# A graph layer on one core: the first messages ahead of a later pair's sum, and a read-back that ends twelve steps beyond the last chunk

## The chip, the core and the metric

The kernel runs on one core of a Trainium2 chip. The metric is the device time of one execution in microseconds (us). A change of less than 0.2% (about 8.5 us here) is taken as no change.

The core has five engines that each work through a queue of their own in order: TensorE (PE, with its weight loads shown as PEld), VectorE (DVE), ScalarE (ACT), GpSimd (POOL) and SyncE (SP, which here issues most DMAs). They wait for each other through semaphores.

## The reference

The layer takes 12,500 nodes of 128 features and 412,500 edges, sorted by `dst`. The part that matters:

```python
h = jnp.maximum(_layernorm(x, axis=-1), 0.0)
h = h @ W_in2f
Wij = ssp(f_ij @ W_f1 + b_f1) @ W_f2 + b_f2      # ssp(z) = softplus(z) - log 2
Wij = Wij * rcut_ij[:, None]
x_ij = h[idx_j] * Wij                            # idx_j = dst: sorted
agg = segment_sum(x_ij, idx_i, 12500)            # idx_i = src: in no order
out = ssp(agg @ W_o1 + b_o1) @ W_o2 + b_o2
return x + out
```

Every edge makes one message of 128 numbers, and the messages are summed by `src`, which comes in no order.

## The kernel before

**Chunks and steps.** The edges are cut into 806 chunks of 512. One step of the main loop (`step(k, units)`) finishes chunk k and starts work on later ones. It writes the order of every engine's queue by hand. Of one chunk's work, the parts that this text needs:

- `hidden` (L653, L656, L657): for a pair of chunks, PE makes z = f·W_f1, and ACT takes |z| and its exponential. There is one PSUM buffer for z. `hidden_log` (L662) is ACT's logarithm, and `hidden_end` (L668) is DVE's sum that ends the softplus of the pair; it is the "pair's sum" of the title, and it frees z for the next pair.
- `blocks`, `rank`, `rank_end` (L673, L692, L697, L717 to L721): a running count on PE, from which DVE works out the row ("slot") of a table that each message goes to. PE's L725 and L692 follow DVE's L697 of the chunk before.
- `window` (L744), `pick` (L772), `picked` (L780): DVE marks, PE gathers and ACT scales the node rows, which gives `hg`.
- `bias` (L757) and `value` (L764): the filter values `v`. ACT's L757 for a later chunk waits for the message that frees its buffer.
- `message` (L789, L791, L795): DVE multiplies v and hg into `o`, and POOL sends it to the table with four indirect DMAs of 128 rows. There are four `o` buffers, of two chunks each; L789 opens one, and waits until the DMAs that last read it are done.

**Segments and read-back.** The chunks are cut into seven segments (352, 160, 120, 56, 56, 32 and 30 chunks), each with a table of its own in HBM. When a segment's last chunk is 9 steps past, a `Collect` reads its table back in units: `load` (L833, an SP DMA), `compare` (L844, DVE), `add` (L857, PE, one unit later) and, after every four blocks of 128 nodes, `keep` (L880, DVE), which adds PE's sum to `agg`. There is one PSUM buffer for that sum. A unit is 3 to 6 tiles of 128 slots.

**When the units run.** Ahead of the loop a plan spreads the units of the first six segments evenly over the steps, with a common end:

```python
at = [seg.c1 + 9 for seg in segs[:-1]]
end = NCH + 6
```

Each segment gets a rate in tiles a step, so that its units fill the steps from its start to the end (or to the next start, where the rate is higher). The loop runs until the last unit's step, beyond chunk 805 if need be. In such steps there is no message, only read-back. After the loop the last segment, whose table is complete only when POOL is done, is read back, and each group of four blocks goes through `finish` (L410 to L434), which makes the output.

**The order within a step** before the change: `rows`, loads, `blocks`, **`end`** (L668), **`window`** (L744), **`message`**, `keep`, `value`, `pick`, `bias`, `picked`, `compare`, `rank`, `hidden`, `log`, `add`, `rank_end`. L668 comes in every second step.

Of the kernel before, what the change touches and what calls it, by code (L numbers as in the profile page):

```python
# [36 lines left out]
def ceil_div(a, b):  # L37
    return -(-a // b)
# [3 lines left out]
def gnn_kernel(  # L42
# [36 lines left out]
    NCH = ceil_div(n_edges, CH)  # L79
# [438 lines left out]
    with tc.tile_pool(name="edge", bufs=2) as edge, tc.tile_pool(  # L518
# [367 lines left out]
        LG, LW, LR, LZ = 12, 6, 6, 4  # L886

        def of(k):
            return groups[k // NCHUNK], k % NCHUNK
# [6 lines left out]
        made = {}  # L896

        def part(name, upto, make):

            for j in range(made.get(name, -1) + 1, min(upto, NCH - 1) + 1):  # L900
                make(*of(j))
                made[name] = j

        def pairs(make):
            return lambda g, c: None if c % 2 else make(g, c)
# [22 lines left out]
        def group(j):  # L928
            if j not in groups and j < NG:
                groups[j] = Group(j)  # L930

        def ranks(j):

            if 0 <= j < NCH:
                g, c = of(j)
                g.rank(c)
                yield
                g.rank_end(c)

        def step(k, units=()):  # L940

            def has(j):
                return 0 <= j < NCH

            group((k + LG) // NCHUNK)
            part("rows", min(k + LW, 2 * k + 3, NEXT if k < NEXT - 3 else NCH), rows)
            for c, u in units:
                c.load(u + AHEAD)  # L950

            part("blocks", min(k + LR + 1, 2 * k + 1), blocks)
            part("end", min(k + LZ - 2, made.get("log", -1)), pairs(hidden_end))
            part("window", k + 2 if k > 0 else k + 1, window)
            if has(k):
                g, c = of(k)
                g.message(c, vs.pop(k), hgs.pop(k))
            for c in owed:
                c.keep()
            owed.clear()  # L960
            if has(k + 1):
                g, c = of(k + 1)
                vs[k + 1] = g.value(c, bs.pop(k + 1))
                ps = psum.tile([P, QT, P], F32, name="picked", tag="v", bufs=3)
                g.pick(c, ats.pop(k + 1), ps)
            if has(k + 2):

                bs[k + 2] = of(k + 2)[0].bias(of(k + 2)[1])
            if has(k + 1):
                hgs[k + 1] = g.picked(c, ps)  # L970
            for c, u in units:
                c.compare(u)
            upto = max(made["rank"], min(k + LR, 2 * k + 1))
            ready = [ranks(j) for j in range(made["rank"] + 1, upto + 1)]
            made["rank"] = upto
            for r in ready[:1]:
                next(r, None)
            part("hidden", k + LZ, pairs(hidden))
            part("log", k + LZ - 1, pairs(hidden_log))
            for c, u in units:  # L980
                if summed:
                    summed[0].add(summed[1])
                summed[:] = c, u
            for r in ready:
                for _ in r:
                    pass
# [18 lines left out]

        at = [seg.c1 + 9 for seg in segs[:-1]]
        work = [sum(seg.tiles(b) for b in range(NBLK)) for seg in segs[:-1]]
        end = NCH + 6
        rate = {}
        while len(rate) < len(at):  # L1010
            n = len(at) - len(rate)
# [3 lines left out]
            end = at[j]  # L1015
# [9 lines left out]
        i, k = 0, todo[0][0]  # L1025
# [43 lines left out]
        with tc.manual_schedule():  # L1069
# [27 lines left out]
            for k in range(-1, max(NCH, max(units) + 1)):  # L1097
                for seg, d in zeros.get(k, ()):
                    seg.clears.append(nc.sync.dma_start(*d).ins.name)
                now = units.get(k, ())  # L1100
                for c, u in now:
                    if u == 0:
                        for i in range(AHEAD):
                            c.load(i)
                step(k, now)

                for m in h:
                    next(m, None)
                if k > NEXT - 3:
                    next(aside, None)  # L1110
# [101 lines left out]
```

## Time and profile before

| | |
|---|---|
| median of 9 runs | 4232.86 us (4226.41 to 4244.69) |
| the profiled execution | 4232.43 us, of which span 4230.6 us |
| busy: PE, DVE, ACT, POOL | 3388.0, 3376.9, 2682.3, 3100.6 us |
| POOL's 3224 indirect DMAs | 961 ns each |
| granted TensorE clock | 0.82 of full in the mean |

The page of the profile gives the busy time of each engine, the costliest groups of instructions (line, engine, operation, what is written from what, how often, busy time, mean of one, and the idle time before them with what ended it), and the chain that ended last. The timeline has one row for an instruction or a run of equal ones: start and length in us, engine and line, and in brackets the idle time ahead of it and what ended that. A row may stand for several instructions (x2). An instruction's printed length is longer than the space that it takes in a queue: VectorE's 0.68 us rows stand 0.60 us apart.

### The profile page before, as it was taken

Reading aid. Unit: us, or ns where it says so; the run is one execution under the profiler, and the core shown is the slowest. Engines: PE = TensorE matmul, PEld = TensorE weight load, DVE = VectorE, ACT = ScalarE, POOL = GpSimd, SP = SyncE. Lnnn points to the kernel's source line nnn. Section 1 sums busy time; section 2 is a strip of 40 time slices with the busy share of each in tenths; the row PEclk is TensorE's granted clock in tenths of the full one; section 3 lists DMA queues with packets and bytes.
Section 4 is the critical chain, followed back from the end, with each engine's and each line's share of the span. In section 5 each row is a group of like instructions: output and inputs, shape, how many; then the busy total and the mean of one; then the engine's idle time right before and its main releaser. Section 6 shows DMA issues by size and latency. Waiting matters only on the chain. (4 is left out here: it accounts for less than half of the span.)

```text
span 4230.6 us, 71871 instructions
## 1 busy us (share of the span) xinstructions
PE 3388.0 (80%) x21576; PEld 2598.7 (61%) x21576; DVE 3376.9 (80%) x6726; ACT 2682.3 (63%) x5490; POOL 3100.6 (73%) x3244
## 2 busy tenths in 40 slices
PE   6777776767787767778888888888888888888878
PEld 4444454444454445467777777777776777767777
DVE  7877766776666666678888888888988998999988
ACT  6676666666666666666666666665666666666635
POOL 5777777777777777777777777777777777777760
PEclk8677666676656665589999999999999999999999
DMA  6656556555444454467787777887778778877667
GB/s 175 202 180 198 176 168 183 156 153 162 130 118 127 121 165 124 112 182 218 235 268 206 219 212 210 254 241 212 213 231 246 231 203 261 240 198 217 191 188 232
DMA packets 515581, 820.80 MB, mean 194 GB/s; under 512 B 177074, under 2 KB 312870, under 8 KB 515186
## 3 DMA queue, kind: packets, MB, share of 16 engines
q1 hardware_dynamic: 411586, 602.85, 50.5%
q0 software_dynamic: 103168, 213.15, 15.3%
q8 instruction: 176, 2.88, 0.3%
q14 instruction: 219, 1.79, 0.1%
q10 hardware_dynamic: 432, 0.13, 0.0%
HBM read 419.09 MB, written 396.64 MB: 193 GB/s over the span
## 5 line engine op out<-in xcount | busy, mean ns | idle before, releaser
L795 POOL DMA_INDIRECT slots<-o,slot x3224 | 3097.4, 961 | 1011.3 <-issue 793.4
L764 PE MATMUL v<-wf,r 128*128 128x128 f32 x6448 | 1138.2, 333 | 336.3 <-ACT v L757 335.1
L764 PEld LDWEIGHTS v<-wf,r 128*128 128x128 f32 x6448 | 1009.4, 238 | 639.4 <-ACT v L757 632.2
L757 ACT ACTIVATE v<-bf 128x512 f32<-128x512 f32 x804 | 478.4, 595 | 1381.0 <-DVE o L791 1378.5
L857 PEld LDWEIGHTS acc<-to,m 128*128 128x128 f32 x8132 | 1050.1, 207 | 344.0 <-DVE agg L880 140.3
L857 PE MATMUL acc<-to,m 128*128 128x128 f32 x8132 | 1125.4, 296 | 115.8 <-DVE agg L880 76.9
L780 ACT ACTIVATE hg<-picked,rcut 128x128 f32<-128x128 f32 x3224 | 908.1, 363 | 59.0 <-PE picked L772 56.4
L653 PE MATMUL z<-f,wf 20*128 20x512 f32 x1612 | 551.8, 760 | 342.2 <-DVE r L668 315.3
L668 DVE SCALAR_TENSOR_TENSOR r<-z,nbf,a 128x1024 f32<-128x1024 f32 x403 | 516.5, 1282 | 314.3 <-ACT a L662 313.0
L844 DVE TENSOR_TENSOR to<-count_ps,m 128x512 f32<-128x512 f32 (+3 forms) x824 | 640.5, 803 | 54.3 <-DMA m<-slots 36.0
L697 DVE TENSOR_REDUCE top<-free 128x4 f32<-128x392 f32 x806 | 447.7, 555 | 203.3 <-PE free L692 201.8
L791 DVE TENSOR_TENSOR o<-v,hg 128x512 f32<-128x512 f32 x806 | 548.3, 680 | 22.8 <-ACT hg L780 21.7
L744 DVE TENSOR_TENSOR at<-count_ps,rel 96x512 bf16<-96x512 f32 x806 | 544.8, 676 | 0.0
L653 PEld LDWEIGHTS z<-f,wf 20*128 20x128 f32 x1612 | 150.0, 214 | 526.2 <-issue 259.7
L662 ACT ACTIVATE a<-a,half 128x1024 f32<-128x1024 f32 x403 | 467.8, 1161 | 0.0
L656 ACT ACTIVATE a<-z,bf 128x1024 f32<-128x1024 f32 x403 | 455.6, 1130 | 5.4 <-PE z L653 5.4
L673 DVE TENSOR_TENSOR inb<-count_ps,blk 128x392 f16<-128x392 f32 x806 | 444.8, 552 | 0.0
L657 ACT ACTIVATE a<-a 128x1024 f32<-128x1024 f32 x403 | 425.9, 1057 | 12.8
L772 PE MATMUL picked<-near,at 96*128 96x128 bf16 x3224 | 377.9, 250 | 4.0 <-DVE at L744 3.9
L725 PE MATMUL free<-inb,rest_of 128*128 128x392 f16 x806 | 320.8, 398 | 12.8 <-DVE top L697 12.7
L772 PEld LDWEIGHTS <-at 96*128 96x128 bf16 x3224 | 305.2, 115 | 34.9 <-DVE at L744 4.5
L692 PE MATMUL free<-inb,after 128*128 128x392 f16 x806 | 318.0, 395 | 5.0 <-DVE used L731 3.4
(108 smaller groups left out, 1135.6 us busy)
## 6 DMA issues: line engine op xcount, KB each, us to landing
m<-slots SPq DMA_DIRECT2D x311, 387.0 KB
m<-slots SPq DMA_DIRECT2D x317, 258.0 KB
rel<-rel_d SPq DMA_DIRECT2D x202, 384.0 KB
m<-slots SPq DMA_DIRECT2D x172, 322.5 KB
slots<-o,slot POOLq DMA_INDIRECT x3224
slots<-zero SPq DMA_DIRECT2D x96, 387.0 KB
slots<-zero SPq DMA_DIRECT2D x64, 516.0 KB
f<-in_f_t SPq DMA_DIRECT2D x404, 80.0 KB
```

The source lines that it names most:

```text
L653: nc.tensor.matmul(z[:, k, :], wf1[rows, :], self.f[rows, :], start=True, stop=True)
L662: nc.scalar.activation(a, a, AF.Ln, bias=half, scale=0.5)
L668: nc.vector.scalar_tensor_tensor(r, z, nbf1, a, op0=ALU.max, op1=ALU.add)
L744: nc.vector.tensor_tensor(at, prow_ps.to_broadcast([WP, CH]), self.rel[:, c, :], op=ALU.is_equal)
L757: nc.scalar.activation(v, spread(bf12, QT), AF.Copy)
L764: nc.tensor.matmul(v[:, i, :], r[:, i * P:(i + 1) * P], wf2, start=False, stop=True, skip_group_check=True)
L772: nc.tensor.matmul(ps[:, i, :], at[:, i * P:(i + 1) * P], near, start=i == 0, stop=i == QT - 1, skip_group_check=True)
L780: nc.scalar.activation(hg[:, i, :], ps[:, i, :], AF.Copy, scale=self.rcut[:, j:j + 1])
L791: nc.vector.tensor_mul(o[:, :, :P], v, hg)
L795: put = nc.gpsimd.indirect_dma_start(out=views[j % VIEWS], out_offset=bass.IndirectOffsetOnAxis(ap=self.slot[:, j:j + 1], axis=0), in_=o[: ...
L844: nc.vector.tensor_tensor(to[:, :n, :], count_ps[:, None, :].to_broadcast([P, n, P]), self.m[u][:, :n, P:].to_broadcast([P, n, P]), op=ALU ...
L857: nc.tensor.matmul(self.acc[b // QT][:, i, :], m[:, j, :P], to[:, j, :], start=t == 0, stop=t == self.seg.tiles(b) - 1)
```

## The change

Two edits. In steps 0 to 3 `end` goes behind `window` and `message`; as L668 comes in every second step, two L668 move (those of steps 0 and 2), each past one L744 and one message. And the plan's end goes from NCH + 6 to NCH + 12, which gives every segment a rate of 8.45 tiles a step, where segments 4 and 5 had 8.71 and the others 8.54; the last unit runs in step 818 and not in 813.

```diff
             part("blocks", min(k + LR + 1, 2 * k + 1), blocks)
-            part("end", min(k + LZ - 2, made.get("log", -1)), pairs(hidden_end))
+            early_on = k < 4
+
+            def end():
+                part("end", min(k + LZ - 2, made.get("log", -1)), pairs(hidden_end))
+
+            if not early_on:
+                end()
             part("window", k + 2 if k > 0 else k + 1, window)
             if has(k):
                 g, c = of(k)
                 g.message(c, vs.pop(k), hgs.pop(k))
+            if early_on:
+                end()
             for c in owed:
                 c.keep()
...
-        end = NCH + 6
+        end = NCH + 12
```

## The prediction, made before the changed kernel ran

> **What bounds the kernel now.** I read the costliest groups of the page first, then the waits, then the timeline at the two ends, where the edits are.
>
> ```profile
> L795 POOL DMA_INDIRECT slots<-o,slot x3224 | 3097.4, 961 | 1011.3 <-issue 793.4
> ```
>
> POOL spends 961 ns on each of 3224 DMAs and then 0.30 us on the next issue: 1.263 us apart, 5.05 us a chunk. From its first DMA at 29.60 to the end of its last at 4112.68 there are 4083.1 us, or 1.2665 us for each. So POOL paces the middle, and time is to be had or lost at only two places: before POOL runs without a break, and after it ends.
>
> The start (timeline):
>
> ```profile
> 21.26 1.14 ACT L780 ACTIVATE hg<-picked,rcut 128x128 f32<-128x128 f32 x4 [5.11 <-PE picked L772]
> 26.76 1.28 DVE L668 SCALAR_TENSOR_TENSOR r<-z,nbf,a 128x1024 f32<-128x1024 f32 x1 [6.47 <-ACT a L662]
> 28.63 0.68 DVE L791 TENSOR_TENSOR o<-v,hg 128x512 f32<-128x512 f32 x1
> 29.60 1.13 POOL L795 DMA_INDIRECT slots<-o,slot  x1 [25.61 <-DVE o L791]
> ...
> 42.05 0.96 POOL L795 DMA_INDIRECT slots<-o,slot  x1 [1.45 <-DVE o L791]
> ...
> 63.02 0.96 POOL L795 DMA_INDIRECT slots<-o,slot  x1 [1.07 <-DVE o L791]
> ```
>
> The first message's inputs are there at 22.40, but it stands behind an L668 for which DVE sits idle 6.47 us. The last row is as important: POOL still waits for message 6, at 63.02, and only from there runs unbroken. What counts is when message 6 comes, not message 0.
>
> The far end (timeline of all engines):
>
> ```profile
> 4090.13 0.69 DVE L791 TENSOR_TENSOR o<-v,hg 128x512 f32<-128x512 f32 x1 [0.47 <-ACT hg L780]
> ...
> 4093.56 0.69 DVE L880 TENSOR_TENSOR agg<-agg,acc 128x512 f32<-128x512 f32 x1 [0.94 <-PE acc L857]
> 4094.16 1.28 DVE L844 TENSOR_TENSOR to<-count_ps,m 128x512 f32<-128x512 f32 x2
> 4094.30 2.05 PE L857 MATMUL acc<-to,m 128*128 128x128 f32 x16 [0.78 <-DVE agg L880]
> ...
> 4107.72 0.69 DVE L880 TENSOR_TENSOR agg<-agg,acc 128x512 f32<-128x512 f32 x1 [0.95 <-PE acc L857]
> ...
> 4111.72 0.96 POOL L795 DMA_INDIRECT slots<-o,slot  x1 [0.30 <-issue]
> ...
> 4116.68 3.77 SPq L833 DMA_DIRECT2D m<-slots  x5
> ...
> 4120.10 0.42 DVE L880 TENSOR_TENSOR agg<-agg,acc 128x256 f32<-128x256 f32 x1 [1.25 <-PE acc L857]
> ...
> 4120.73 1.86 DVE L844 TENSOR_TENSOR to<-count_ps,m 128x512 f32<-128x512 f32 x3
> ```
>
> The last message ends at 4090.82. What follows on DVE is read-back of segment 5: two units a step, in which DVE's L880 waits 0.94 us for PE's one accumulator and PE waits for L880. The last segment's first compare is at 4120.73, without idle time ahead of it: directly behind DVE's read-back. The chain through POOL (last DMA, load at 4116.68) was ready by then, at most a moment before. So both chains meet at 4120.73, DVE's is the one that binds, and the 110 us behind it are the same in both kernels.
>
> How far DVE runs ahead of POOL decides the rest. Message rows laid beside POOL's rows, four to a chunk, give a lead of 25 to 28 us up to step 564. There the four `o` buffers cap it: L789 waits for POOL, the last time for 2.91 us at message 560 and 0.03 at 564. From there it falls to 17.1 us at message 805, and L789 is not among the waits:
>
> ```profile
> DVE r L668 <- ACT a L662: 44.0, 60, 1.7
> DVE to L844 <- DMA m<-slots: 26.1, 19, 4.3
> DVE to L844 <- PE acc L857: 12.8, 18, 1.7
> ```
>
> (waits of DVE from 2845 to 4090 us). DVE's own rows, 90 to 96% busy, set the time of message 805.
>
> **Edit 1, the start.** Two L668 move. In step 0 the L744, L789 and message 0 fill idle time ahead of L668. Message 0 then waits for hg alone: it ends at about 23.1, and POOL starts at 23.4, 6.2 us earlier. L668 stays at 26.76 to 28.04, since ACT's L662 ends at 26.73 as before. Then L697 follows at 28.05 and not at 29.99: DVE is 1.94 us earlier, and message 1 ends at 33.64, not 35.58. In step 2 the second L668 goes behind message 2: it would run at 38.56 to 39.83, against 39.23 to 40.50, so it gains only 0.67. PE's L653 of pair 6 cannot start before that L668 has read z:
>
> ```profile
> 40.65 1.13 PE L653 MATMUL z<-f,wf 20*128 20x512 f32 x4
> ```
>
> Behind it on PE's queue stand L725 and L692 of the next count, for which DVE's next L697 waits. With 1.13 us, L653 ends at 41.0, and that L697 comes at 41.54, not at 42.83: 1.3 us earlier. At half clock the same four rows take 2.07 us (50.60), and 0.3 us is left. From message 3 on the order is the old one, with DVE nearly without gaps, so message 6 comes 1.3 us earlier, and with it all of POOL's remaining chain and DVE's capped lead. POOL merely waits longer between chunks 0 and 1. ACT and PE queues keep their order; ACT's L757, which waited for messages 0 and 2, is released sooner. SP's loads keep theirs too. I take −1.3; the bounds are −6.2 (message 0's own gain) and 0.
>
> [...] By half clock the term would be −0.3.
>
> **Edit 2, before the last message.** The plan moves work towards the end. By step 564 the new plan is at unit 24 of segment 1, where the old one is at 29. What was put off before 564 brings nothing, since POOL's cap binds there. From 564 on, the old plan has 225 steps up to unit 0 of segment 5 in step 789, then 16 steps of segment 5 up to step 805. The new one has 230, with five more units of four tiles, and 11. Five steps of segment 5 become five steps of the older kind. A segment 5 step takes 4.82 us (messages 791 to 799 end 4021.05 and 4059.58: 38.53 / 8). An older step without units takes 3.42 us: over 82 pairs of steps from 564 to 800 (those over 10.6 us, with a segment's end or new columns, left out) time is 6.84 us a pair and 1.01 us for each us of L844. So 5 × 4.82 = 24.1 us go, 5 × 3.42 + 5 × 0.60 = 20.1 us come: −4.0 us at message 805. Bounds: nothing, as DVE already waits for ACT 60 times here and freed time may turn into more of that; and −9.0 us, if all ten units put off (ten L844 at 0.60 and five L880 at 0.60) count.
>
> **Edit 2, behind the last message.** The units that run beyond step 805 go from 16 to 26. The ten more are of four tiles, two a step, like those in the rows above: L880 to L880 is 2.83 us (4093.56 to 4107.72 is 14.16 for five). Five more steps: +14.15 us. Nothing hides them: POOL is done by then, and DVE and PE wait for each other in turn. Bounds: 9.0 us if only DVE's rows counted, 18.6 if each step took the 3.72 us of the six-tile steps (4114.44 to 4118.16). The ten loads that move past the last chunk on SP's queue stand ahead of the last segment's loads, which therefore come later too; they are still issued three units ahead, so I cost them at nothing. Were that cover gone, one load's 4.05 us (4116.68 to 4120.73) at most would be added.
>
> **Sum.** 14.15 − 1.3 − 4.0 = +8.85 us at the first compare of the last segment, and at the end. The profiled execution takes 4232.43, 0.4 under the median: 4232.43 + 8.85 = 4241.3, and from the median 4232.86 + 8.85 = 4241.7. I forecast 4241.7, 0.21% slower: just over what a measurement can tell, so the cases on both sides have weight.
>
> **Rivals.**
>
> *The put-off work is won back (no change).* If DVE gains more before message 805, the extra steps are paid. With −9.0 in place of −4.0 the sum is +3.9, 4236.7 us. It decides from 4.4 us of savings up (14.15 − 1.3 − 8.45). For it: DVE is at 90 to 96%, and the L880 of segment 5 fall into a full queue. Against it: the fit gives an L880 hardly any price (0.1 us), as DVE often waits nearby anyway.
>
> *The savings vanish in ACT's waits (slower by more).* L668 waits for L662 in about every second step. If the freed time becomes such a wait, 14.15 − 1.3 leaves +12.9: 4245.7 us. Against it: time does follow L844 at 1.01.
>
> *POOL's chain decides (faster).* If DVE were done first, the last segment would start by POOL's last DMA: 4.00 us from its end to the load, at most 4.05 to the compare. With −1.3 to −6.2 of POOL the time is 4231.6 to 4226.7. It needs 14.15 us won before message 805 beyond POOL's own gain, which DVE shares; the bound is 9.0.
> [...]
>
> *Edit 1 does nothing.* If message 6 is as late as before, the sum is 14.15 − 4.0 = +10.2: 4243.0. This lies within the forecast's own range.
>
> **Chances.** The forecast, +8.5 to +11: 0.40. Savings lost: 0.20. Won back: 0.36. POOL decides: 0.04, of which 0.03 go beyond 0.2%. So slower 0.60, same 0.37, faster 0.03. The likeliest case's own range is 4241 to 4244; the whole range is 4235 to 4248: below, the won-back case with 1.5 us more from the start; above, all savings and the start's gain lost (4247.0) and 1 us of spread between medians.
>
> **What would show it.** In the profile after: the first L795 near 23.4, POOL's wait for message 6 near 61.7, its last DMA ending near 4111.4; message 805 ending near 4085.5 and a lead near 21; 13 steps of read-back behind it, most 2.83 us long; the first compare of the last segment near 4129.6, with no wait for its load. The forecast is wrong if message 805 comes before 4080 or if the steps behind it are shorter than 2.83 us: the read-back would then hardly end later. It is wrong as well if the 110 us of the last segment change.

## The result: 0.39% slower, and the profile after

The changed kernel takes 4253.31 us in the median of 17 runs (4244.25 to 4262.57), beside 4234.31 us for the kernel before. The ratio, taken between the means, is 1.0039, with a 95% interval from 1.0032 to 1.0047: some 16.5 us slower (13.5 to 19.9); the medians lie 19.0 us apart. The forecast was 8.85 us slower, and 4248 us was the upper end of its range. The profiled execution of the changed kernel took 4262.19 us, which is near the upper end of its runs; I come back to that.

Behind L950 the line numbers of the changed kernel are 8 higher than before. The lines that matter here (L653 to L880) keep theirs.

**The start** (timeline of after, a row for an instruction: start, length, engine and line, and the idle time ahead of it with what ended it):

```profile
22.65 0.69 DVE L791 TENSOR_TENSOR o<-v,hg 128x512 f32<-128x512 f32 x1 [1.42 <-ACT hg L780]
23.64 1.13 POOL L795 DMA_INDIRECT slots<-o,slot  x1 [19.65 <-DVE o L791]
...
34.69 0.58 PE L772 MATMUL picked<-near,at 96*128 96x128 bf16 x4 [2.29 <-DMA near<-h]
...
35.96 0.57 DVE L697 TENSOR_REDUCE top<-free 128x4 f32<-128x392 f32 x1 [2.21 <-PE free L692]
...
40.72 1.27 DVE L668 SCALAR_TENSOR_TENSOR r<-z,nbf,a 128x1024 f32<-128x1024 f32 x1
...
42.13 2.00 PE L653 MATMUL z<-f,wf 20*128 20x512 f32 x4 [2.10 <-DVE r L668]
...
66.34 0.96 POOL L795 DMA_INDIRECT slots<-o,slot  x1 [0.61 <-DVE o L791]
```

POOL starts 5.96 us earlier (23.64, before 29.60), near the 6.2 us of the forecast. Eleven microseconds later PE waits 2.29 us for the node rows of chunk 2. PE's count stands behind that on its queue, DVE's next L697 waits for the count, and it starts at 35.96, where it started at 35.74 before. So what was won at message 0 is gone by then. The second moved L668 starts at 40.72 (before 39.23), and PE's L653 behind it follows at 42.13 (before 40.65). POOL waits for message 6 at 66.34, not at 63.02.

**The far end** (timeline of after):

```profile
4105.42 0.69 DVE L791 TENSOR_TENSOR o<-v,hg 128x512 f32<-128x512 f32 x1 [0.47 <-ACT hg L780]
...
4108.85 0.69 DVE L880 TENSOR_TENSOR agg<-agg,acc 128x512 f32<-128x512 f32 x1 [0.94 <-PE acc L857]
...
4111.68 0.69 DVE L880 TENSOR_TENSOR agg<-agg,acc 128x512 f32<-128x512 f32 x1 [0.94 <-PE acc L857]
...
4114.95 0.96 POOL L795 DMA_INDIRECT slots<-o,slot  x1 [0.30 <-issue]
...
4149.45 0.42 DVE L880 TENSOR_TENSOR agg<-agg,acc 128x256 f32<-128x256 f32 x1 [1.25 <-PE acc L857]
...
4150.08 1.86 DVE L844 TENSOR_TENSOR to<-count_ps,m 128x512 f32<-128x512 f32 x3
```

The last message ends at 4106.11, and the first compare of the last segment starts 43.97 us later (before: 29.91 us). Most steps between are 2.83 us apart, with the wait of 0.94 us for PE's accumulator that the prediction showed. POOL is done at 4115.91, 34 us before that compare. What follows takes 110.4 us (before 109.9).

**Between the ends.** The next two lines are from the busy time by stretches, the first of before, the second of after: stretch, its length, busy time of PE, PEld, DVE, ACT and POOL (with instructions), granted clock, DMA share, GB/s. The stretch reaches from about message 564 to about message 805.

```profile
2865.00:4091.00 1226.00, 1051.38 (x7917) 877.66 (x7915) 1107.40 (x2093) 762.88 (x1561) 930.23 (x971) 0.93 0.75 219
```

```profile
2867.00:4106.00 1239.00, 1062.87 (x7871) 887.76 (x7871) 1103.99 (x2085) 763.54 (x1561) 939.09 (x980) 0.92 0.74 216
```

DVE works 3.4 us less, and the stretch is 13 us longer. DVE's waits in it (us in total, times, longest), first of before from 2864 to 4091 us, then of after from 2867 to 4106:

```profile
DVE r L668 <- ACT a L662: 43.8, 59, 1.7
DVE to L844 <- PE acc L857: 12.6, 17, 1.7
DVE top L697 <- PE free L692: 10.4, 14, 1.4
```

```profile
DVE r L668 <- ACT a L662: 49.6, 66, 2.1
DVE to L844 <- DMA m<-slots: 23.8, 17, 3.9
DVE top L697 <- PE free L692: 16.8, 18, 2.0
```

The wait for L662 is the one to look at: it is 40.6 to 45.5 us in the four profiles of the old plan (before, and three kernels told below) and 47.3 to 49.6 us in the three of the new one. The wait for L692 differs as much within the old plan (10.4 to 16.5 us), so its 16.8 tells nothing. In after, DVE's lead over POOL has fallen to 5.1 us by message 805 (before 17.1). POOL even waits for messages near the end, once for 1.27 us.

### The profile page after: what moved, and what is told of

Read it like the earlier page. It is cut to its first block, busy times and chain, and to the rows that moved or that the text cites. A ratio compares the mean times of both kernels' runs of the same rounds, so it can differ in the third digit from the quotient of the medians.

```text
span 4260.5 us, 71909 instructions
## 1 busy us (share of the span) xinstructions
PE 3393.9 (80%) x21576; PEld 2609.5 (61%) x21576; DVE 3377.5 (79%) x6726; ACT 2685.1 (63%) x5490; POOL 3099.4 (73%) x3244
## 5 line engine op out<-in xcount | busy, mean ns | idle before, releaser
L653 PE MATMUL z<-f,wf 20*128 20x512 f32 x1612 | 548.0, 755 | 362.9 <-DVE r L668 326.1
L668 DVE SCALAR_TENSOR_TENSOR r<-z,nbf,a 128x1024 f32<-128x1024 f32 x403 | 516.5, 1282 | 313.3 <-ACT a L662 310.6
L697 DVE TENSOR_REDUCE top<-free 128x4 f32<-128x392 f32 x806 | 447.8, 556 | 230.8 <-PE free L692 229.6
L744 DVE TENSOR_TENSOR at<-count_ps,rel 96x512 bf16<-96x512 f32 x806 | 544.9, 676 | 0.0
L653 PEld LDWEIGHTS z<-f,wf 20*128 20x128 f32 x1612 | 149.1, 212 | 547.2 <-issue 314.0
L662 ACT ACTIVATE a<-a,half 128x1024 f32<-128x1024 f32 x403 | 467.7, 1161 | 0.0
L692 PE MATMUL free<-inb,after 128*128 128x392 f16 x806 | 317.5, 394 | 8.0 <-DVE used L731 5.3
```

The source lines that it names most:

```text
L653: nc.tensor.matmul(z[:, k, :], wf1[rows, :], self.f[rows, :], start=True, stop=True)
L662: nc.scalar.activation(a, a, AF.Ln, bias=half, scale=0.5)
L668: nc.vector.scalar_tensor_tensor(r, z, nbf1, a, op0=ALU.max, op1=ALU.add)
L744: nc.vector.tensor_tensor(at, prow_ps.to_broadcast([WP, CH]), self.rel[:, c, :], op=ALU.is_equal)
```

## The experiments

Each kernel was timed against the kernel before on the same chip, with one profiled execution. Single profiles scatter: at the usual clock (0.82 to 0.83 for the whole) the start of POOL's unbroken run lies at 62.2 to 64.0 us in all kernels without the whole first edit, and message 805 of the old plan between 4084.9 and 4095.1. Seven of the eighteen runs fell on chips on which the kernel before itself takes 5751 to 5839 us, with a granted clock of 0.71 to 0.73 for the whole; they are told last, as little of them can be compared.

### Which edit costs

**The first edit alone** (`end = NCH + 6` kept).

> The first edit alone (end back at NCH + 6). Theory A, the start is lost as in the profile after: message 6 comes 3 us later (POOL at 66 and not at 63.0), POOL's chain ends 2 to 3 us later, and the time is 2 to 3 us (0.05 to 0.07%) above before. Rival, as predicted: message 6 comes 1.3 us earlier, and the time is 1 us lower.

Measured: 1.0005 [0.9996, 1.0014]. The first DMA of POOL starts at 23.16, message 2 ends at 40.19, message 3 at 45.83, message 4 at 53.44, and POOL has message 6 at 64.12 (before 41.77, 45.53, 51.77, 63.02). The first edit moves message 0 by 6 us and the kernel by nothing that can be measured.

**The plan alone** (the loop's order as before, `end = NCH + 12`).

> The second edit alone (end at NCH + 12, the order of the steps as before). Theory A, nothing is won before the last message: 13 steps of read-back behind it in place of 8, at 2.83 us, 14 us (0.33%) above before, and message 805 not earlier than before. Rival, as predicted: message 805 comes 4 us earlier, 10 us (0.24%) above before. Second rival, the new plan itself slows VectorE ahead of message 805: over 16 us (0.38%).

Measured: 1.0046 [1.0033, 1.0060]. The 43.93 us between the last message and the first compare are those of after. The plan alone costs as much as both edits together, so the cost is in the plan.

**Only one of the two sums moved** (plan as before):

```diff
-            early_on = k < 4
+            early_on = k < 2          # first sum only; the other kernel: 2 <= k < 4
```

> Of the first edit, only step 0: message 0 goes ahead of the sum of chunks 2 and 3, the sum of step 2 stays where it was; end at NCH + 6. Theory A: the 1.9 us that VectorE gains up to message 1 are eaten by the node rows of chunk 2, which land late behind the first scatters, so message 6 comes within 0.5 us of before and the time is the same. Rival, the gain of 1.9 us lasts: message 6 near 61.1, 2 us (0.05%) faster.

> Of the first edit, only step 2: message 2 goes ahead of the sum of chunks 4 and 5; end at NCH + 6. Theory A: that sum ends 1.5 us later, TensorE's z of the next pair waits for it, the count behind that comes 1.5 to 2.5 us later, and message 6 comes 1.5 to 3 us later; time 1.5 to 3 us (0.04 to 0.07%) above before. Rival: message 2 gains 1.2 us and nothing behind it moves, time as before.

Measured: 1.0000 [0.9991, 1.0009] and 1.0008 [0.9998, 1.0017]. With the first sum alone message 0 comes 6.3 us earlier, but message 2 ends at 42.22, 0.45 us later than before. With the second alone message 2 is 1.2 us earlier (40.55), and message 3 0.7 us later (46.20, before 45.53): the message that went ahead of L668 is paid back one message later, as PE's L653 and the count behind it wait for L668. POOL has message 6 at 63.36 and 63.71, inside the scatter.

### What happens before the last message

**The plan alone once more**, beside the three kernels that follow.

> The plan alone once more, beside the three others on the same chip: 1.0046 of before, as in its first run. For its steps 632 to 690: 290 us again, if these are the plan's own and not that one execution's (284 to 286 if it was the execution's).

Measured: 1.0054 [1.0040, 1.0068]; steps 632 to 690 take 291.1 us, so the 290.1 us of its first run are the plan's own. I can now put the executions of one plan together. The old plan's are those of before and of the three kernels with only the first edit or part of it; the new plan's are after and the two of the plan alone. Means in us, by the ends of the messages:

| steps | old plan (4) | new plan (3) | difference |
|---|---|---|---|
| 564 to 632 | 361.4 | 356.1 | -5.3 |
| 632 to 690 | 284.6 | 291.7 | +7.1 |
| 690 to 744 | 275.9 | 278.7 | +2.8 |
| 744 to 805 | 304.0 | 303.9 | 0.0 |
| sum | 1225.8 | 1230.4 | +4.6 |

Between 632 and 690 both plans read back the same 493 tiles, in 97 and 96 units. DVE's busy time over all steps falls from 1107.4 to 1103.1 us; its idle time rises from 118.6 to 127.6. The loss between 632 and 690 is clear of the scatter (283.9 to 285.6 against 290.2 to 293.9). The sum is not: the old plan's four lie between 1222 and 1229 us, and most of the +4.6 is after's own execution (1238). The two of the plan alone have 1225 and 1228, with 4.7 us less work of DVE and 5.2 us more idle time. So the profiles show no gain; how much was lost is read from the whole times, further down.

**The last part of the plan alone.**

```diff
             end = at[j]
+        for i in (4, 5):
+            rate[i] = sum(work[4:]) / (NCH + 12 - at[4])
```

> Only the read-back of segments 4 and 5 (from step 753 on) is spread as if it ended at step 818; up to step 752 the plan is that of before, odd and even steps too. Thirteen steps behind the last message and not nine: +11.3 us at 2.83 a step. By the prediction's way of counting some 4 us are won between 753 and 805, so +7 us, 1.0017 of before. If nothing is won before the last message wherever the units come from, +11 us, 1.0027. Steps 632 to 690 take 284 to 286 us as before either way.

Measured: 1.0032 [1.0019, 1.0044], which is 13 us (8 to 19). There are only twelve steps behind the last message, one less than I had written: the first compare comes 38.26 us after the message, 8.4 us more than the 29.9 before. By the runs, then, all that lies behind the last message is paid in full, and nothing is won ahead of it (13 - 8.4 = +5 us, -0.4 to +10). The profiled execution says otherwise: it is the quickest of the six (4230.44 us), and in it steps 564 to 805 take 1219 us, some 7 less than in the old plan, with 302.1 us for steps 744 to 805. One execution does not outweigh the other five.

**A shift of one step**, in steps 630 to 689 alone; once with the old plan, once with the new one:

```diff
-                todo.append((int(pos), c, u))
+                todo.append((int(pos) + (630 <= int(pos) < 690), c, u))
```

> The plan as before, but what it gives out in steps 630 to 689 comes one step later, so that units of odd steps stand in even steps there: 32.2 us of compare in odd and 39.3 in even steps between 632 and 690, where before has 40.2 and 32.2. Nothing else is changed, and the steps behind the last message stay nine. Theory 'odd and even steps differ' (7.05 us a pair of steps, 0.73 per us of compare in the odd step, 1.31 in the even one): steps 632 to 690 take 3.4 to 8 us more than the 284 to 286 of before, and the whole is 4 to 8 us slower (some 4232 to 4236 against 4227.7). Theory 'only the number of units counts': no change within 0.1%.

> The new plan without the first edit, and again what it gives out in steps 630 to 689 comes one step later: 37.4 us of compare in odd and 33.4 in even steps between 632 and 690, where the new plan has 34.9 and 37.4. Theory 'odd and even steps differ': steps 632 to 690 take 3.5 to 7 us less than the 290 to 294 of the new plan, and some 2 us come back behind 690, so the whole is 2 to 5 us faster than the plan alone, which was 18 us slower than before (so 1.0031 to 1.0041 of before). Theory 'only the number counts': the same as the plan alone (1.0046).

Measured: the old plan with the shift 1.0045 [1.0031, 1.0058], the new plan with it 1.0059 [1.0045, 1.0073]. The old plan's case is the strongest single finding. Its stretch (from the same view as above) has DVE's busy time of before, but is 15 us longer:

```profile
2865.00:4106.00 1241.00, 1066.45 (x7910) 892.78 (x7911) 1106.33 (x2092) 763.04 (x1561) 935.82 (x978) 0.92 0.73 216
```

Steps 632 to 690 take 294.6 us (284.6), steps 690 to 744 282.7 us (275.9). Not one unit was added; sixty steps' units came one step later, at a price of 19 us, more than either theory allowed. In the new plan the shift wins 3 us in steps 632 to 690 (287.3), just under what was expected, and loses 2.7 and 2.8 us in the stretches on either side, so the whole does not follow.

**More units in odd or in even steps.** At this point my theory was odd against even steps. L668 stands in the even ones. Two pairs of steps of before show why (timeline of DVE; each has three units of six tiles in two steps):

```profile
3354.32 0.94 DVE L844 TENSOR_TENSOR to<-count_ps,m 128x768 f32<-128x768 f32 x1
3355.18 0.55 DVE L697 TENSOR_REDUCE top<-free 128x4 f32<-128x392 f32 x1
3355.65 0.55 DVE L673 TENSOR_TENSOR inb<-count_ps,blk 128x392 f16<-128x392 f32 x1
3357.80 1.28 DVE L668 SCALAR_TENSOR_TENSOR r<-z,nbf,a 128x1024 f32<-128x1024 f32 x1 [1.59 <-ACT a L662]
...
3411.67 1.81 DVE L844 TENSOR_TENSOR to<-count_ps,m 128x768 f32<-128x768 f32 x2
3413.40 0.55 DVE L697 TENSOR_REDUCE top<-free 128x4 f32<-128x392 f32 x1
3413.87 0.55 DVE L673 TENSOR_TENSOR inb<-count_ps,blk 128x392 f16<-128x392 f32 x1
3414.55 1.28 DVE L668 SCALAR_TENSOR_TENSOR r<-z,nbf,a 128x1024 f32<-128x1024 f32 x1
```

In the first pair one unit stands ahead of L668 and two behind it; DVE arrives early and waits 1.59 us for ACT. In the second two stand ahead of it, and there is no wait. The first pair takes 10.42 us and the second 8.95 us, and so they do in the other executions of the old plan, within 0.01 us. So the steps were taken in pairs, and a larger or smaller share of each pair's units given to the odd step:

```diff
-                todo.append((int(pos), c, u))
+                odd = int(pos) // 2 * 2
+                todo.append((max(at[i], odd if pos - odd < 1.4 else odd + 1), c, u))
```

(By the plan's positions 1.4 gives 70% to the odd step, 0.8 gives 40%, 1.7 gives 85%. Counted in tiles from the traces, in steps 564 to 804, the odd steps have 50% before, and 58, 46 and 65% in these three: the 40% is the smallest of the three moves.)

> The plan of before with its steps taken in pairs: of the units that fall into a pair, those of the first 70% of it go into the odd step, the rest into the even one (before: 50%). Number and order of the units, and the nine steps behind the last message, stay. Compare in odd and even steps from 564 to 805: 178 and 126 us, where before has 153 and 151. Theory 'odd and even steps differ': the fit gives 14 us less up to message 805; as POOL's last DMA then comes last, at most 8 us of it shows at the end, so 0.998 to 0.9995 of before. Theory 'only the number of units counts': 1.000. Theory 'the old plan is a lucky one, and any change of its steps costs': 1.002 to 1.005, as for the shift in steps 630 to 689.

> The same the other way: 40% of a pair goes into the odd step. Compare in odd and even steps from 564 to 805: 140 and 165 us. Theory 'odd and even steps differ': 8 us more up to message 805 by the fit, more if as large as for the shift in steps 630 to 689; 1.002 to 1.005. Theory 'only the number counts': 1.000. Theory 'any change of the steps costs': 1.002 to 1.005 too, so this run counts only beside the one before it.

> 85% of a pair goes into the odd step: 198 and 107 us of compare, 39 even steps of 121 without or with one small unit only, and some odd steps with four units. Theory 'odd and even steps differ': by the fit 26 us less up to message 805, but POOL's chain ends last, so 0.998 to 0.9995 as for 70%; if four units in a row meet the one accumulator or their loads, more waits for these than are won, 1.001 to 1.004. Theory 'only the number counts': 1.000.

Measured: 70%: 1.0030 [1.0018, 1.0042]. 40%: 1.0000 [0.9991, 1.0009]. 85%: 1.0083 [1.0070, 1.0096]. My theory fell: more in odd steps costs, and a little more in even steps costs nothing. "Any other placing costs" fell with it, by the 40%. DVE's waits with 70% (2863 to 4095 us) show what takes the place of the wait for ACT:

```profile
DVE r L668 <- ACT a L662: 45.9, 52, 2.5
DVE to L844 <- PE acc L857: 27.7, 27, 2.7
```

The wait for L662 did not fall (43.8 before), and the compare now waits 27.7 us for PE's sums (before 12.6): 47 steps now have three or four units, where 29 had before. That these fill the three `to` buffers between DVE and PE is my reading; no run took it apart. The pair of steps above is thus a true reading of one pair and no rule for the plan.

Across all of these, DVE's work in steps 564 to 805 hardly differs, and its idle time does (stretch and busy time from the same view, idle time by subtraction):

| kernel | stretch | DVE busy | DVE idle | ratio of the whole |
|---|---|---|---|---|
| before | 1226 | 1107.4 | 118.6 | 1 |
| 40% in odd steps | 1223 | 1107.3 | 115.7 | 1.0000 |
| 70% in odd steps | 1232 | 1106.1 | 125.9 | 1.0030 |
| 85% in odd steps | 1256 | 1110.0 | 146.0 | 1.0083 |
| shift in steps 630 to 689 | 1241 | 1106.3 | 134.7 | 1.0045 |
| last part of the new plan | 1219 | 1101.1 | 117.9 | 1.0032 |
| new plan, first run | 1226 | 1103.7 | 122.3 | 1.0046 |
| new plan, second run | 1227 | 1101.6 | 125.4 | 1.0054 |
| new plan with the shift | 1227 | 1101.4 | 125.6 | 1.0059 |
| after | 1239 | 1104.0 | 135.0 | 1.0039 |

One rival is not settled. PE's busy time rises with the stretch, at no more matmuls: 1051.38 us before, 1062.87 in after and 1066.45 with the shift (the lines shown), while the granted clock falls from 0.93 to 0.92. So a part of these 13 to 15 us may be PE's rows at a lower clock; whether that makes DVE wait or comes of the waiting, no run here separates. It is not the reason that nothing was won: the two executions of the plan alone have 1049.8 and 1053.9 us of PE at 0.93, and their stretch is no shorter either.

### Runs on chips with other times

**A table of arrangements, tested blind.** From the profiles at the usual clock, but that of 85% in odd steps, I fitted the time of a pair of steps to its place, the number of units and of ended groups in it and in the pair before. Three kernels were built to test it, with

```diff
-                todo.append((int(pos), c, u))
+                todo.append((int(pos + 0.5 * (564 <= pos < 690)), c, u))
```

in the new plan, and, in the other two, 1.5 steps from 690 to 788 (new plan) and 1 step from 592 to 620 (old plan). A further line keeps the units in their order.

> The new plan without the first edit; what it would give out between steps 564 and 690 comes half a step later, so that some units move on by one step (431 units up to the last message and 14 steps behind it, as in the new plan). Theory 'the arrangement of a pair of steps decides' (a table over the twelve profiles at the usual clock but that of 85% in odd steps: time of a pair of steps by its place in the run, the number of units and of ended groups in its two steps and in the two before): 13 us less before the last message than the new plan, of which 6.5 between 564 and 632 and 5 between 632 and 690, so 1.002 of before and not 1.005. Theory 'only the number of units counts': 1.005, as the plan alone. Theory 'any other placing than the planned one costs': 1.007 or more.

> The new plan without the first edit; what it would give out between steps 690 and 788 comes one and a half steps later. The same 431 units up to the last message and 14 steps behind it. The table by arrangement: 11 us more before the last message than the new plan, 5 of them between 690 and 744, so 1.0075 of before. By the number of units: 1.005.

> The plan of before; only what it gives out between steps 592 and 620 comes one step later. 436 units before and nine steps behind the last message, as before. The table by arrangement: 6 us less before the last message, all of it between 564 and 632; as POOL's chain then ends last, at most 3 us of that shows in the whole: 0.9990 to 1.000. By the number of units: 1.000. 'Any other placing costs': 1.002 or more.

Measured, where before takes 5750.59 us: 1.0041 [1.0020, 1.0063], 1.0039 [1.0016, 1.0062] and 1.0018 [0.9990, 1.0046]. The table wanted 24 us between the first two, and they are alike. But there POOL stands waiting for DVE, whose lead is 0.3 us at message 564: steps 564 to 805 take 1703 and 1678 us (1226 at the usual clock), and the plan alone was not run beside them. The table is neither confirmed nor refuted for the usual clock.

**No early clears, with the first edit.** The first store of zeros to a table comes six steps later (`t0, i = 6, 0` for `0, 0`).

> The first edit alone (end at NCH + 6), and the zero stores of the first table begin in step 6 and not in step 0 (they stand closer afterwards). Theory: the node rows of chunk 2 come late since their load queues behind a 387 KB zero store and behind the first scatters. Without the zero stores it lands 1.5 us sooner or more, TensorE no longer waits for it at the second pick, and VectorE keeps its gain of 1.9 us up to message 2 (near 38.7 in place of 40.2); message 6 comes 1 to 2 us earlier than in the first edit alone (63.85). Rival: the scatters alone hold the load up; nothing changes at the second pick. Time within 0.1% of before in both.

Measured: 1.0011 [0.9987, 1.0035], beside 5838.82 us. Message 2 ends at 38.68, where it ended at 40.19 with the clears, and at 39.92 with the clears on the same chip (the next kernel, which starts like this one). The last packet of the rows of chunk 2 comes at 31.20 and not at 32.27, and PE, which waits 2.94 us for them in the next kernel, does not wait for them here. So the stores of zeros do hold these rows up, by 1.07 us in this pair of profiles. By message 6 (65.43) the two chips can no longer be compared.

**Two accumulators behind the last chunk.** In the changed kernel PE's sum takes its buffer from those of `v` once there are no more chunks:

```diff
-    self.acc[b // QT] = psum.tile([P, QT, P], F32, name="acc")
+    self.acc[b // QT] = (psum.tile([P, QT, P], F32, name="acc_v", tag="v", bufs=3)
+                         if kept.get("late") else psum.tile([P, QT, P], F32, name="acc"))
```

> The changed kernel, but units that run beyond the last chunk take their accumulator from the three buffers that v and picked use until then, so TensorE need not wait for VectorE's keep. Theory: the 2.83 us of such a step is the wait of each for the other; it falls to 2.0 to 2.1 us (TensorE's sixteen matmuls), the stretch from message 805 to the first compare of the last segment falls from 44.0 to 33 to 35 us, and the time is 9 to 11 us below the changed kernel's. Rival: the loads (258 KB each, two a step) set the pace; the step stays at 2.8 us, and the time that of the changed kernel, 0.4% above before.

Measured: 1.0020 [0.9994, 1.0047], beside 5838.82 us. The steps behind the last message shrink from 2.83 to 2.54 us (L880, which is L882 in this kernel, at 5709.94 and, ten steps on, at 5735.33), and DVE still waits 0.65 us for PE in each. With one buffer these steps take 2.83 us on this chip too. So the single buffer is only 0.3 us of the 0.94; even so, by this figure thirteen steps would win back some 4 us, which no run shows in the whole time.

**The plan one step later, and the last part alone.** The first is the old plan with `seg.c1 + 10` and `NCH + 7`; the second is the kernel of the last part above.

> The plan of before moved as a whole by one step (segments start 10 steps after their last chunk, end at NCH + 7; the first edit left out). The same units in the same groups, but a group that stood in an odd step stands in an even one. Theory, that a unit costs VectorE more in an even step (where its sum L668 stands) than in an odd one (1.31 against 0.73 us for each us of compare): steps 564 to 632 take 3 to 5 us less than before's 361, and steps 632 to 690 take 3 to 5 us more than before's 285. Rival: only the number of units counts; both stretches as before within 1 us. The time: one more step behind the last chunk, 2 to 4 us above before.

> The plan of before up to step 757, and only the last two segments that are read back in the loop (4 and 5) spread to NCH + 12: 7.9 tiles a step for them. Six more units behind message 805 (24, not 18), so about 10.5 us more from message 805 to the first compare. Theory P, that in the changed kernel the gain ahead of message 805 was lost to where the units fell before step 690: here nothing falls differently there, VectorE is 4 to 5 us earlier at message 805, and the time is 5 to 7 us (0.12 to 0.16%) above before. Rival N, that less work ahead of message 805 makes VectorE no earlier: 10 to 11 us (0.25%) above before.

Measured beside 5838.82 us: 5856.98 us in a single run, and 1.0008 [0.9984, 1.0031]. POOL waits for DVE (its lead is 0.3 us at message 564 in both), so neither says anything on the question; the second was run again.

## Why the prediction was wrong, step by step

**Behind the last message: right.** Forecast +14.15 us for five more steps of 2.83; measured 43.97 - 29.91 = +14.06, and 43.93 and 43.92 in the two runs of the plan alone. The loads cost nothing, POOL was long done, and the stretch behind the first compare stayed the same (110.4 and 109.9 us; 108 to 112 over all profiles at the usual clock).

**The start: -1.3 forecast, 0 measured** (1.0005, interval -1.7 to +5.9 us). The first steps came as forecast: 23.64 for POOL's start (23.4), the first L668 at its old place (26.98, before 26.76). Two things were missing. Message 1 came 1.84 us earlier (33.07 for 34.91), but DVE's work behind it has to wait for PE (2.21 us at L697), and PE for the node rows of chunk 2 (2.29 us). The prediction said that SP's loads keep their order, and never asked whether these rows land earlier. They land later: their last packet at 33.10 us (before 31.53; 32.35 with the first edit alone), with POOL's first four DMAs now running ahead of them. And L668 of step 2 was costed as if it came 0.67 us earlier; it came 1.49 us later, at 40.72. The clock alone is not the reason: PE's four rows of L653 behind that L668 took 2.00 us in after, at a granted clock of 0.53 (before: 1.13 us at 1.00, and 2.07 us at 0.50 for the rows at 50.60), but 1.13 us with the first edit alone, and that one gained nothing either. The bound of 0 that the prediction gave was right, as was its rival on the first edit.

What holds these rows up is shown in part. The clears do, in one pair of profiles: without them the rows land at 31.20 us, 1.07 earlier than with them on the same chip, although POOL's four DMAs run ahead there too. That POOL's four DMAs do so as well is my reading of the later landing; no run here took them away while keeping the rest.

**Ahead of the last message: -4.0 forecast, +2 to +9 measured. This is the step that failed.** With the 14.06 us behind the message taken off the whole differences, 16.5 - 14.1 = +2 us is left for after (interval -0.6 to +5.8), and 19.4 - 14.1 = +5 and 22.8 - 14.1 = +9 for the two runs of the plan alone. The prediction gave an average price to a moved unit (24.1 us go, 20.1 come) and bounded the saving by nothing and 9.0.

DVE's work did fall by 4.3 us, which is about that size. But the time did not follow it: DVE's idle time rose by at least as much. The part of it that stands clear of the scatter is L668's wait for ACT's L662, 43.5 us in the mean of the old plan and 48.1 in that of the new one: +4.6. It is not the whole account, as in the new plan with the shift that wait is 45.5 us and the time no better. DVE shares a cycle of two steps with ACT and PE, and how long it waits there changes with the step that each unit falls into. That was shown by the shift of one step (the same units, +19 us) and by 70 and 85% in odd steps (+13 and +35 us; 40% costs nothing). The new rate moves most units to other steps, also between 632 and 744, where the prediction saw the same work and put no cost: that stretch alone lost 9.9 us (8.7 in the two executions of the plan alone). That the places of the units are the reason there too is inferred from the shift, not shown by itself. The lower bound of the saving should have been below nothing.

The rival "the savings vanish in ACT's waits" (+12.9) was nearest, in its number and in its cause: the wait that grew is the one that it names. Its price was one-sided, like the step's: it allowed a saving to vanish, not to become a loss, and it kept the 1.3 us of the start. "Won back" (+3.9) and "POOL decides" needed savings that are not there.

**What stays open.** Why an arrangement is good or bad, and how much of it is PE's clock. "Odd against even" was refuted as a rule. A table by neighbouring pairs was fitted afterwards, without the 85%, and its blind test could not be read. And the profiled execution of after is about 9 us slower than its median, nearly all of it ahead of message 805; the plan alone had that message at 4085.65 and 4089.39, so its 4106.11 is that execution's. Nor would those two have settled the matter: they lie where the forecast had message 805 (4085.5), but so does one execution of the old plan (4084.9). The comparison of single profiles would have told a wrong story here, in either direction.

No version found beats the kernel before; 40% in odd steps equals it.

## What to carry to other kernels

Here DVE was busy for 1107.4 of 1226 us and waited in a cycle with two other engines, and the price of a moved piece of work was not its duration: sixty steps' units, one step later, cost 19 us. In such a place bound the price from both sides of nothing, and test it by moving the same work by one step. Of a message that is made early, ask which load behind it is not brought forward: message 0 came 6 us earlier here, PE then waited 2.29 us for the rows of chunk 2, and the first edit alone stayed at 1.0005. What stood alone behind the last message was costed to a tenth of a microsecond by counting rows: 14.15 us forecast, 14.06 measured.

## What the runs showed of the hardware

Many pairs of steps take the same time in every execution of one plan: of the 120 pairs between messages 565 and 805, 30 agree within 0.02 us in all four executions of the old plan, and 59 in at least three. Others jump: 53 differ by more than 0.5 us in some execution, such as the pair at step 662 with 9.68 us in one and 8.32 in three others. And the kernel before took 4226 to 4234 us at the usual clock but 5751 and 5839 us on two other chips; there the granted clock was 0.71 to 0.73 (here 0.82) and DVE, not POOL, set the pace (its lead was 0.3 us at message 564), so an edit's worth there says nothing about its worth here.
